# Cross attention and a routed FFN on one core: the query weights are centred before they are folded into the key weights, and the start of the program is put in another order

## The chip, the cores and the metric

The kernel runs on one core of one Trainium2 chip. A core has five engines that run side by side, each through its own queue of instructions in program order: TensorE (PE, matrix products; its weight loads are shown apart as PEld), VectorE (DVE), ScalarE (ACT), GpSimd (POOL) and SyncE (SP, which here only issues DMAs; ACT and POOL issue DMAs too). The metric is the device time of one execution in microseconds (us); smaller is better. All data are float32 unless said otherwise.

## The reference, cut to what matters

```python
def xattn(query, context, w_q, w_kv, w_out, b_out):      # 16 heads of 64
    q = query @ w_q
    k, v = jnp.split(context @ w_kv, 2, axis=-1)
    ...
    attn = jax.nn.softmax(jnp.einsum('bhqd,bhkd->bhqk', q, k) * HEAD_DIM ** -0.5, axis=-1)
    ...
    return out @ w_out + b_out

x = x + xattn(layernorm(x), ctx_768, w_q, w_kv, w_out, b_out)
x = x + moe_ffn(layernorm(x), router_w, w1, w2, w3, sw1, sw2, sw3)
```

`x` is 64 batches of 128 tokens of 128 features, `ctx_768` 64 batches of 77 keys of 96 features, `w_q` 128 x 1024, `w_kv` 96 x 2048. The FFN has eight experts, of which each token takes two, and a shared expert. The layer norm subtracts the mean of a token's 128 features and divides by their deviation.

## The kernel before, in words

**Folded weights.** The kernel never forms q and k. For each head it multiplies the key weights by the query weights once, at the start (`folded`, L231 to L244): `wkq` is 96 x 128 per head, so that keys times `wkq` times the raw tokens gives the scores. The layer norm's mean is taken out of the weights rather than out of the tokens: `fold_keys` (L246 to L259) takes from each row of a folded head its mean over the 128 token features, and scales by 1/8 on the way. The deviation is applied later, as the scale of the exponential (L366). In the same way `fold_values` (L261 to L263) multiplies value weights by output weights. The weights come in two quads `q` of four pairs of heads; a quad is two DMAs (`wk[q]` and `wq[q]`, L104) and 8 products of 64 rows, the even heads into one PSUM bank and the odd heads into another. A float32 product is two PE instructions in the profile. So a quad shows as 16 PE instructions at L237, and on DVE as twice (reduce L250, scale L251, subtract L252), once for each bank; each bank holds 96 x 512.

**Units.** The work on a group of four batches is cut into units of one batch and eight heads. For a unit, `scores` (L343 to L362) multiplies tokens by keys (L351, four PE instructions) into a PSUM tile of two banks that exists once, DVE takes the largest (L360) and subtracts it (L362) and so frees the tile; ACT takes the exponential (L366); DVE sums and inverts (L373, L375) and POOL multiplies (L381 to L385). `keys(k)` makes folded keys for two heads (L334, four PE instructions) and ACT copies them out of PSUM (L341). After that come transposes (L420), products with the values (L403, L430), and the FFN's steps, which are put between the units by a plan written out by hand.

**The start of the program**, which the change touches. SP issues `wk` of both quads, then the first group's keys `cT` (L115), tokens `xg` (L117), transposed tokens `xgT` (L128), and then further inputs and `wo`. ACT issues `wq` of both quads, `wv` of both (L104) and `bo_sb` (L149). POOL makes the identity `ident`, then the constant `mhalf` (L163), then many other constants. The arithmetic then stands in this order for every engine:

```python
    more_constants()
    fold_keys(0)
    fold_keys(1)
    stats(0)
    for k in range(4):
        keys(k)
    start_unit(0, lambda: [keys(k) for k in range(4, 8)])
    start_unit(1, lambda: fold_values(0), lambda: fold_values(1), lambda: residual(0))
```

`stats(0)` is the first group's layer norm statistics on DVE (L277 to L281) and POOL (L283). `start_unit(n, ...)` issues the scores of unit n, then what is handed to it, then the unit's exponential and weights. `keys(0)` to `keys(3)` need the heads 0 to 7, that is both banks of quad 0; `keys(4)` to `keys(7)` need quad 1. ACT loads its function table once ahead of its first arithmetic, a copy at L341.

After the two first units the program goes on unit by unit; further keys, values, FFN and routing work are laid into it, and the last tenth is FFN work on blocks of routed tokens whose inputs and answers go through DRAM.

Of the kernel before, what the change touches and what calls it, by code (L numbers as in the profile page):

```python
# [8 lines left out]
F32 = mybir.dt.float32  # L9
BF16 = mybir.dt.bfloat16  # L10
I32 = mybir.dt.int32
AF = mybir.ActivationFunctionType
ALU = mybir.AluOpType
AX = mybir.AxisListType

B, NQ, D = 64, 128, 128
NKV, DC = 77, 96
# [14 lines left out]
G = 4  # L32
# [30 lines left out]
SCALE = HD ** -0.5  # L63
# [3 lines left out]
def xattn_moe_kernel(  # L67
# [17 lines left out]
    nc = tc.nc  # L85
    PSUM = bass.MemoryType.PSUM

    const = ctx.enter_context(tc.tile_pool(name="const", bufs=1))
    grp = ctx.enter_context(tc.tile_pool(name="grp", bufs=2))
    dram = ctx.enter_context(tc.tile_pool(name="dram", bufs=1, space=bass.MemoryType.DRAM))  # L90
    small = ctx.enter_context(tc.tile_pool(name="small", bufs=3))
# [8 lines left out]
    def weights_of(engine, w, q, n, name):  # L100

        to = ffn.tile([128, WALL], F32, tag="w", name=f"{name}_{q}", bufs=2 * QUAD)
        to = to[:, : 4 * n].rearrange("p (m d) -> p m d", d=n)
        engine.dma_start(out=to, in_=w[:, 4 * q : 4 * (q + 1), :])  # L104
        return to

    wk, wq, wv, wo = {}, {}, {}, {}
    for q in range(2):
        wk[q] = weights_of(nc.sync, wkT, q, DC, "wk")
        wq[q] = weights_of(nc.scalar, wqT, q, D, "wq")  # L110

    def load_inputs(g):
        bs = slice(g * G, (g + 1) * G)
        cT = grp.tile([DC, G, NKV], F32, tag="cT", name=f"cT_{g}", bufs=2)
        nc.sync.dma_start(out=cT, in_=ctxT[:, bs, :])  # L115
        xg = grp.tile([128, G, D], F32, tag="xg", name=f"xg_{g}", bufs=2)
        nc.sync.dma_start(out=xg, in_=x[bs].rearrange("b t d -> t b d"))  # L117
        return xg, cT

    def load_first_keys(g):  # L120

        cM = grp.tile([DC, G // 2, 3 * KM], F32, tag="cM", name=f"cM_{g}", bufs=2)
        nc.sync.dma_start(out=cM, in_=ctxM[:, g * G // 2 : (g + 1) * G // 2, :])
        return cM

    def load_transposed(g):
        xgT = grp.tile([D, T], F32, tag="xgT", name=f"xgT_{g}", bufs=2)
        nc.sync.dma_start(  # L128
            out=xgT.rearrange("d (b t) -> d b t", t=NQ), in_=xT[:, g * G : (g + 1) * G, :]
        )  # L130
        return xgT

    def load_last_keys(g):

        cR = grp.tile([DC, 2 * G * KS], F32, tag="cR", name=f"cR_{g}", bufs=1)
        nc.sync.dma_start(out=cR.rearrange("c (b k) -> c b k", k=KS), in_=ctxR[:, g * G : (g + 2) * G, :])
        return cR

    inputs, transposed = {0: load_inputs(0)}, {0: load_transposed(0)}
    first_keys, last_keys = {0: load_first_keys(0)}, {0: load_last_keys(0)}  # L140
    for q in range(2):
        wv[q] = weights_of(nc.scalar, wvT, q, DC, "wv")
# [13 lines left out]
    def keys_room(name):  # L156

        return grp.tile([D, QUAD * WALL], F32, tag="kx", name=name)

    ident = const.tile([128, 128], F32, name="ident")  # L160
    make_identity(nc, ident)
    mhalf = const.tile([128, G], F32, name="mhalf")
    nc.gpsimd.memset(mhalf, -0.5)  # L163

    ats = []
    for i in range(NAT):
# [24 lines left out]
    def iota(to, pattern, base, step):  # L191
        nc.gpsimd.iota(to, pattern, base=base, channel_multiplier=step, allow_small_or_imprecise_dtypes=True)

    def more_constants():
        for e in range(E):
            nc.gpsimd.memset(rank[:, :, e : e + 1], float(E - e))
        nc.gpsimd.memset(upto, 0.0)
        for e in range(E):
            nc.gpsimd.memset(upto[:, e, : e + 1], 1.0)
            nc.gpsimd.memset(first_row[:, e : e + 1], float(e * rows))  # L200
        iota(block_no, [[1, nb]], 0, 0)
        iota(block_row, [[128, nb]], 0, 1)
        nc.gpsimd.memset(ones, 1.0)
        nc.gpsimd.affine_select(before, ones, [[1, 128]], ALU.is_gt, 0.0, base=0, channel_multiplier=-1)
        iota(dest, [[1, 2 * G]], nb * 128, 2 * G)
        for h in hrs:
            nc.gpsimd.memset(h, 0.0)
        nc.gpsimd.memset(nobody, 0.0)
        nc.gpsimd.memset(nobody[:, D : D + 1], NOWHERE)
        for to in sent:  # L210
            nc.sync.dma_start(out=to[E * rows :, :], in_=nobody)
# [12 lines left out]
    wkq_sb = const.tile([DC, NH, D], F32, name="wkq_sb")  # L224
# [3 lines left out]
    def bank(name, p=128):  # L228
        return ps_g.tile([128, 512], F32, tag="g", name=name)[:p]

    def folded(q, left, right, name):  # L231

        pws = [bank(f"{name}_{q}_{odd}", DC) for odd in range(2)]
        for m in range(4):
            for odd in range(2):
                half = slice(HD * odd, HD * (odd + 1))
                nc.tensor.matmul(  # L237
                    pws[odd][:, m * D : (m + 1) * D],
                    left[q][half, m, :],
                    right[q][half, m, :],  # L240
                    start=True,
                    stop=True,
                )
        return [(slice(8 * q + odd, 8 * (q + 1), 2), pw.rearrange("p (h d) -> p h d", d=D)) for odd, pw in enumerate(pws)]  # L244

    def fold_keys(q):  # L246

        for hs, pw in folded(q, wk, wq, "pwq"):
            mean = small.tile([DC, 4], F32, tag="wmean", name=f"wmean_{hs.start}", bufs=2)
            nc.vector.tensor_reduce(mean, pw, AX.X, ALU.add)  # L250
            nc.vector.tensor_scalar(mean, mean, SCALE / D, None, ALU.mult)  # L251
            nc.vector.scalar_tensor_tensor(  # L252
                wkq_sb[:, hs, :],
                pw,
                SCALE,
                mean.rearrange("p (h o) -> p h o", o=1).broadcast_to([DC, 4, D]),
                ALU.mult,
                ALU.subtract,
            )  # L259

    def fold_values(q):  # L261
        for hs, pw in folded(q, wv, wo, "pwv"):
            nc.scalar.copy(wvo_sb[:, hs, :], pw)  # L263
# [3 lines left out]
    class Norm:  # L267


        def __init__(self, name, src):  # L270
            self.name, self.src = name, src
# [39 lines left out]
    class Attention:  # L311


        def __init__(self, g):
            self.g = g
            self.xg, self.cT = inputs.pop(g)
            self.xgT = transposed.pop(g)
            self.norm = Norm(f"a{g}", self.xg)
            self.kx, self.vo, self.aT, self.sc, self.at = {}, {}, {}, {}, {}

        def residual(self):
            self.x1 = grp.tile([128, G, D], F32, tag="x1", name=f"x1_{self.g}", bufs=NX1)
            nc.gpsimd.tensor_tensor(
                self.x1, self.xg, bo_sb.rearrange("p (o d) -> p o d", o=1).broadcast_to([128, G, D]), ALU.add
            )

        def keys(self, p, i):

            if i == 0:
                self.kx[p] = keys_room(f"kx_{self.g}_{p}")[:, : NH * KP].rearrange("p (h k) -> p h k", k=KP)  # L330
            hs = slice(2 * i, 2 * (i + 1))
            pk = bank(f"pk_{self.g}_{p}_{i}")[:, : 2 * KP].rearrange("p (h k) -> p h k", k=KP)
            for k in range(2):
                nc.tensor.matmul(  # L334
                    pk[:, k].rearrange("p (b k) -> p b k", k=NKV),
                    wkq_sb[:, 2 * i + k, :],
                    self.cT[:, 2 * p : 2 * (p + 1), :],
                    start=True,
                    stop=True,
                )  # L340
            nc.scalar.copy(self.kx[p][:, hs, :], pk)  # L341
# [531 lines left out]
        pairs("values", 4, k)  # L873

    def load_group(g):
        inputs[g] = load_inputs(g)

    def load_first_keys_of(g):
# [8 lines left out]
    for g in range(NG):  # L887
        p = 16 * g
# [24 lines left out]
    g = 0  # L913
# [4 lines left out]
    for g in range(NG - 1):  # L918
        p = 16 * (g + 1)
        routing(g, p, (0, "stats"), (1, "normed"), (3, "transpose"), (4, "logits"), (5, "choose"), (6, "choose_second"))  # L920
    for st in sets:
        for g in range(st.start, min(st.start + st.n, NG - 1)):
            p = 16 * (g + 1)
# [7 lines left out]
    for st in sets[:-1]:  # L931
        p = 16 * (st.start + st.n)
# [6 lines left out]
    for st, after in zip(sets, sets[1:]):  # L939
# [4 lines left out]
        for q, quad in enumerate(quads):  # L944
            p = st.ready + (until - st.ready) * q // (len(quads) - 1)
# [107 lines left out]
    def unit(k):  # L1053
        g, b, t = units[k]
        return attention_of(g), b, t

    def start_unit(k, *between):
        a, b, t = unit(k)
        a.scores(b, t)
        for step in between:  # L1060
            step()
        a.exps(b, t)
        a.weights(b, t)

    more_constants()
    fold_keys(0)
    fold_keys(1)
    stats(0)
    for k in range(4):
        keys(k)  # L1070
    start_unit(0, lambda: [keys(k) for k in range(4, 8)])
    start_unit(1, lambda: fold_values(0), lambda: fold_values(1), lambda: residual(0))
    for k in range(8, 12):
        keys(k)
    load_group(1)
    load_transposed_group(1)
    for i, tag in enumerate(("a", "a", "u", "u")):
# [3 lines left out]
    for k in range(len(units) + 1):  # L1081
# [3 lines left out]
        if k and k % 2 == 0:  # L1085
            a, b, t = unit(k - 1)
# [4 lines left out]
        a, b, t = unit(k)  # L1091
# [87 lines left out]
```

## Time and profile before

| what | value |
|---|---|
| median of 3 runs | 990.72 us (990.32 to 992.84) |
| the profiled execution's own time | 990.29 us |
| its span, first to last instruction | 988.6 us |
| PE / PEld busy | 920.6 us (93%) / 768.4 us (78%) |
| DVE / ACT / POOL busy | 673.3 us (68%) / 651.8 us (66%) / 518.6 us (52%) |
| mean granted TensorE clock | 0.979 of full |
| DMA | 85.76 MB, mean 87 GB/s |

The profiled execution is 1.7 us longer than its span, which is what lies around the first and the last instruction. The page splits the span into 40 slices and gives each engine's busy share of each in tenths. The timeline gives instructions in order of time: start, length in us, engine, line, operation, what it writes and reads, the number of instructions merged into the row, and in brackets how long the engine stood idle before it and what ended that. ACTq and SPq are DMA issues by those engines' queues. The table of groups gives one row for a line and a shape: busy us in all, and mean ns of one instruction, from which an instruction that is new in the program can be priced by its nearest likeness. A mean of one pipelined PE instruction is longer than the step from one to the next; where a step is wanted, it is the length of a merged row divided by its instructions.

### The profile page before, as it was taken

To read this page: it belongs to the slowest core of one execution; us is meant where nothing else is said; L and a number is where in the kernel's file an instruction comes from. 1 tells how busy PE (TensorE), PEld (TensorE's weight loads), DVE (VectorE), ACT (ScalarE), POOL (GpSimd) and SP (SyncE) were. 2 spreads that over 40 slices of the span, in tenths; PEclk is the share of its full clock that TensorE was granted. 3 is DMA by queue.
4 is the path that set the end of the run, shared out by engine and by line. 5 is a ranking of instruction groups with operands and counts; after the bars stand their busy time and mean duration, and the time that the engine had idled before them with its cause. 6 is when DMAs were issued, how large, how long until landed. Compare 5 with 4: busy or idle time off the path is not lost. (4 is left out here: it accounts for less than half of the span.)

```text
span 988.6 us, 18829 instructions
## 1 busy us (share of the span) xinstructions
PE 920.6 (93%) x6103; PEld 768.4 (78%) x6103; DVE 673.3 (68%) x1755; ACT 651.8 (66%) x1417; POOL 518.6 (52%) x688
## 2 busy tenths in 40 slices
PE   7999999999999999999999999999999896689990
PEld 5787877787778878776888888888888775588980
DVE  4566776676767767778686776776676879456552
ACT  4776677676767667675776767666767575456660
POOL 3244563636364544636366375484475556437673
PEclk9999999999999999999999999999999999879995
DMA  5212212212222222122322222123131136623375
GB/s 169 78 59 73 68 41 81 70 54 71 73 70 64 78 70 64 44 88 77 91 76 69 81 84 67 47 84 91 52 95 37 52 111 188 209 61 92 107 221 163
DMA packets 80882, 85.76 MB, mean 87 GB/s; under 512 B 11328, under 2 KB 62912, under 8 KB 80784
## 3 DMA queue, kind: packets, MB, share of 16 engines
q1 hardware_dynamic: 65920, 56.09, 20.7%
q0 software_dynamic: 8864, 18.30, 5.6%
q10 hardware_dynamic: 6000, 10.16, 2.8%
q8 instruction: 49, 0.80, 0.3%
q14 instruction: 49, 0.40, 0.1%
HBM read 48.18 MB, written 36.33 MB: 85 GB/s over the span
## 5 line engine op out<-in xcount | busy, mean ns | idle before, releaser
L334 PEld LDWEIGHTS pk<-cT,wkq_sb 96*128 96x128 f32 x1024 | 157.8, 189 | 70.5 <-issue 42.8
L791 POOL DMA_INDIRECT answers<-y,to x149 | 146.9, 986 | 92.4 <-issue 45.0
L341 ACT COPY kx<-pk 128x308 f32<-128x308 f32 x256 | 104.5, 417 | 129.2 <-PE pk L334 123.9
L334 PE MATMUL pk<-cT,wkq_sb 96*128 96x154 f32 x1024 | 174.9, 294 | 1.4 <-DVE wkq_sb L252 1.0
L351 PE MATMUL ps<-kx,xgT 128*128 128x308 f32 x512 | 156.7, 426 | 11.4 <-DVE sc L362 10.8
L430 PEld LDWEIGHTS py<-vo,aT 128*128 128x128 f32 x1280 | 154.7, 193 | 15.5 <-ACT vo L408 5.3
L430 PE MATMUL py<-vo,aT 128*128 128x128 f32 x1280 | 156.8, 277 | 4.2 <-ACT vo L408 4.0
L629 POOL DMA_INDIRECT sent<-pay,row x128 | 127.2, 994 | 61.7 <-DVE part L619 27.9
L383 POOL TENSOR_TENSOR at<-sc,ri 128x512 f32<-128x512 f32 x64 | 67.3, 1052 | 166.6 <-DVE ri L375 113.0
L408 ACT COPY vo<-pv 64x512 f32<-64x512 f32 x256 | 147.3, 575 | 2.1 <-ACT vn L448 0.4
L403 PE MATMUL pv<-wvo_sb,cM 96*128 96x512 f32 x256 | 131.1, 594 | 1.2 <-DVE hr L507 0.8
L373 DVE TENSOR_REDUCE sm<-sc 128x8 f32<-128x616 f32 x128 | 101.1, 790 | 38.7 <-ACT sc L366 37.8
L366 ACT ACTIVATE sc<-sc,rs_a 128x616 f32<-128x616 f32 x128 | 105.0, 820 | 28.6 <-DVE sc L362 19.6
L351 PEld LDWEIGHTS ps<-kx,xgT 128*128 128x128 f32 x512 | 88.9, 189 | 40.7 <-issue 11.4
L381 POOL TENSOR_TENSOR at<-sc,ri 128x256 f32<-128x256 f32 x128 | 76.8, 623 | 79.3 <-DVE ri L375 31.7
L423 ACT COPY aT<-pa 128x512 f32<-128x512 f32 (+1 forms) x256 | 96.2, 429 | 31.7 <-PE pa L420 27.3
L362 DVE TENSOR_TENSOR sc<-ps,mx 128x616 f32<-128x616 f32 x128 | 102.4, 800 | 12.9 <-DVE mx L360 0.5
L360 DVE TENSOR_REDUCE mx<-ps 128x8 f32<-128x616 f32 x128 | 98.2, 767 | 7.7 <-PE ps L351 6.4
L420 PE MATMUL pa<-ident,at 128*128 128x128 f32 x640 | 92.2, 275 | 0.0
L768 PE MATMUL p<-xT,w 128*128 128x128 f32 x596 | 77.6, 285 | 13.1 <-ACT xT L763 7.2
L768 PEld LDWEIGHTS p<-xT,w 128*128 128x128 f32 x596 | 73.2, 199 | 17.3 <-ACT xT L763 10.1
L420 PEld LDWEIGHTS pa<-ident,at 128*128 128x128 f32 x640 | 75.8, 143 | 11.2 <-issue 10.7
(147 smaller groups left out, 1400.8 us busy)
## 6 DMA issues: line engine op xcount, KB each, us to landing
xb<-sent SPq DMA_DIRECT2D x149, 65.0 KB
last_values<-vn ACTq DMA_DIRECT2D x32, 256.0 KB
vo<-last_values SPq DMA_DIRECT2D x64, 128.0 KB
ya<-answers SPq DMA_DIRECT2D x15, 512.0 KB
xg<-in_x_dram SPq DMA_DIRECT2D x16, 256.0 KB
xgT<-in_xT_dram SPq DMA_DIRECT2D x16, 256.0 KB
parked<-x SPq DMA_DIRECT2D x14, 256.0 KB
yx<-parked SPq DMA_DIRECT2D x14, 256.0 KB
```

What stands on the lines that cost most here:

```text
L334: nc.tensor.matmul(pk[:, k].rearrange("p (b k) -> p b k", k=NKV), wkq_sb[:, 2 * i + k, :], self.cT[:, 2 * p : 2 * (p + 1), :], start=True, ...
L341: nc.scalar.copy(self.kx[p][:, hs, :], pk)
L351: nc.tensor.matmul(ps[:, r, : 4 * NKV].rearrange("p (j k) -> p j k", k=NKV), self.xgT[:, ts], self.kx[p][:, h : h + 4, ks], start=True, st ...
L362: nc.vector.tensor_tensor(at, sc, over_keys(mx), ALU.subtract)
L366: nc.scalar.activation(at, at, AF.Exp, scale=self.norm.rs[:, b : b + 1])
L403: nc.tensor.matmul(pv, self.cM[:, p, KM * r : KM * (r + 2)], wvo_sb[:, h : h + 4, :], start=True, stop=True)
L408: nc.scalar.copy(self.vo[b][rows, 4 * t : 4 * (t + 1), :], pv[rows].rearrange("p (m d) -> p m d", d=D))
L420: nc.tensor.transpose(pa[:, j * NQ : (j + 1) * NQ], keys[:, c : c + 128], ident)
L430: nc.tensor.matmul(py[:, :D], aT[:, m, :], vo[:, m, :], start=(m == 0), stop=(m == NT - 1))
L629: ins = nc.gpsimd.indirect_dma_start(out=sent[st.i], out_offset=bass.IndirectOffsetOnAxis(ap=self.row[:, i : i + 1], axis=0), in_=self.pay ...
L768: nc.tensor.matmul(to[:m, ts], self.w[j][:, c : c + m], self.xT[:, ts], start=True, stop=True)
L791: ins = nc.gpsimd.indirect_dma_start(out=answers[st.i], out_offset=bass.IndirectOffsetOnAxis(ap=self.to[:, j : j + 1], axis=0), in_=self.y ...
```

## The change

1. `wq` is asked for ahead of `wk` in the source (they are on different queues); `mhalf` is made first on POOL, and an exponential of it, whose result nobody reads, is put on ACT's queue between the issues of `wq` and `wv`, so that the table load goes there.
2. On SP's queue the transposed tokens of the first group come ahead of its tokens.
3. A new function `centre(q)` takes the mean out of the query weights before they are folded: reduce, scale and subtract on DVE over 128 x 512 in SBUF, once for each quad. It is the same arithmetic in another place, since the mean of a product's rows is the product with the mean.
4. `fold_keys` then only scales each bank on the way out of PSUM: quad 0 on ACT, quad 1 on DVE.
5. `warm(10)` puts ten products of the identity with itself ahead of the folds on PE; nobody reads them.
6. The fold of quad 1 stands after `keys(0)` to `keys(3)` instead of ahead of them.

```diff
     for q in range(2):
+        wq[q] = weights_of(nc.scalar, wqT, q, D, "wq")
         wk[q] = weights_of(nc.sync, wkT, q, DC, "wk")
-        wq[q] = weights_of(nc.scalar, wqT, q, D, "wq")
+    mhalf = const.tile([128, G], F32, name="mhalf")
+    nc.gpsimd.memset(mhalf, -0.5)
+
+    nc.scalar.activation(small.tile([128, G], F32, tag="shift", name="first_exp"), mhalf, AF.Exp)
...
-    inputs, transposed = {0: load_inputs(0)}, {0: load_transposed(0)}
+    contexts = {0: load_keys(0)}
+    transposed = {0: load_transposed(0)}
+    inputs = {0: load_inputs(0)}
...
+    def centre(q):
+
+        w = wq[q]
+        mean = small.tile([128, 4], F32, tag="wmean", name=f"wmean_{q}", bufs=2)
+        nc.vector.tensor_reduce(mean, w, AX.X, ALU.add)
+        nc.vector.tensor_scalar(mean, mean, 1.0 / D, None, ALU.mult)
+        nc.vector.tensor_tensor(
+            w, w, mean.rearrange("p (m o) -> p m o", o=1).broadcast_to([128, 4, D]), ALU.subtract
+        )
+
     def fold_keys(q):
-
         for hs, pw in folded(q, wk, wq, "pwq"):
-            mean = small.tile([DC, 4], F32, tag="wmean", name=f"wmean_{hs.start}", bufs=2)
-            nc.vector.tensor_reduce(mean, pw, AX.X, ALU.add)
-            nc.vector.tensor_scalar(mean, mean, SCALE / D, None, ALU.mult)
-            nc.vector.scalar_tensor_tensor(
-                wkq_sb[:, hs, :],
-                pw,
-                SCALE,
-                mean.rearrange("p (h o) -> p h o", o=1).broadcast_to([DC, 4, D]),
-                ALU.mult,
-                ALU.subtract,
-            )
+            if q == 0:
+                nc.scalar.mul(wkq_sb[:, hs, :], pw, SCALE)
+            else:
+                nc.vector.tensor_scalar(wkq_sb[:, hs, :], pw, SCALE, None, ALU.mult)
+
+    def warm(n):
+
+        pi = bank("pi")
+        for _ in range(n):
+            nc.tensor.matmul(pi[:, :128], ident, ident, start=True, stop=True)
...
     more_constants()
+    warm(10)
+    for q in range(2):
+        centre(q)
     fold_keys(0)
-    fold_keys(1)
     stats(0)
     for k in range(4):
         keys(k)
+    fold_keys(1)
     start_unit(0, lambda: [keys(k) for k in range(4, 8)])
```

The rest of the diff splits `load_inputs` into a load of keys and a load of tokens; the later groups call the two one after the other, in the order they had.

## Prediction, made before the changed kernel was run

> **What bounds the kernel now.** I read the page's busy shares and 40 slices first, then PE's waits, then the timeline of the first 20 us, because all edits lie there.
>
> ```profile
> PE 920.6 (93%) x6103; PEld 768.4 (78%) x6103; DVE 673.3 (68%) x1755; ACT 651.8 (66%) x1417; POOL 518.6 (52%) x688
> PE   7999999999999999999999999999999896689990
> ```
>
> PE is nine tenths busy or more from the second slice to the 31st. In the waits of PE between 16 and 400 us there is one row:
>
> ```profile
> PE ps L351 <- DVE sc L362: 0.4, 1, 0.4
> ```
>
> This is the wait that ends at 16.02 us. From there PE never waits for another engine before 400 us, so the start counts by the moment at which PE gets there, unit 1's scores, and the work of PE behind that moment is unchanged. What the start gains is carried to the end, unless a later wait is fixed by something else. Later waits exist (PE waits 13 us in 400 to 800 us, 23 us in 800 to 990), but most of them are for engines that PE's own products feed, so I let them move along. The timeline of the start (start, length, engine, line, in brackets the idle time before):
>
> ```profile
> 4.85 3.63 PE L237 MATMUL pwq<-wq,wk 64*96 64x128 f32 x32 [4.85 <-DMA wk<-in_wkT_dram]
> 6.90 0.69 DVE L250 TENSOR_REDUCE wmean<-pwq 96x4 f32<-96x512 f32 x1 [6.90 <-PE pwq L237]
> 7.23 0.33 ACTq L149 DMA_DIRECT2D bo_sb<-in_b_out_dram  x1
> 7.60 1.28 ACT L341 ACT_TABLE_LOAD   x1 [7.60 <-DMA cT<-in_ctxT_dram]
> ...
> 10.09 2.10 PE L334 MATMUL pk<-cT,wkq_sb 96*128 96x154 f32 x14 [0.99 <-DVE wkq_sb L252]
> 10.65 1.99 ACT L341 COPY kx<-pk 128x308 f32<-128x308 f32 x4 [1.77 <-PE pk L334]
> ...
> 14.24 0.79 DVE L360 TENSOR_REDUCE mx<-ps 128x8 f32<-128x616 f32 x1
> 15.07 0.80 DVE L362 TENSOR_TENSOR sc<-ps,mx 128x616 f32<-128x616 f32 x1
> 16.02 1.28 PE L351 MATMUL ps<-kx,xgT 128*128 128x308 f32 x4 [0.44 <-DVE sc L362]
> 17.23 1.99 PE L237 MATMUL pwv<-wo,wv 64*96 64x128 f32 x32
> ```
>
> The reader is to see a chain: weights at 4.85, fold of quad 0 (2.05 to DVE's first reduce), two banks on DVE to 10.03 (3.13), keys from 10.09, their copies, scores to 13.48, then DVE. DVE has quad 1 and the statistics in hand until 14.33, so the maximum starts at 14.24 and the PSUM tile is free at 15.87.
>
> **Part by part, with the new chain.**
>
> Centring adds, for each quad, a reduce, a small scale and a subtract on DVE. The 96x512 reduce took 0.68 (L250), the scale 0.17 (L251), an SBUF 128x512 add 0.70 (L833); from start to start the old trio took 0.73 + 0.20, so 0.73 + 0.20 + 0.70 = 1.62. From 4.85 that ends at 6.47. The trace shows only that both first weight DMAs had landed at 4.85; if `wq` alone landed earlier the start is earlier. Quad 1 is centred to 8.0, beside PE and off the path.
>
> Fold 0 starts at 6.53 (DVE's end to PE's start took 0.06 at 10.03). Its price is the question of `warm`. The same 32 instructions took 3.63 us at 4.85 and 1.99 us at 17.23:
>
> ```profile
> L237 PE MATMUL pwq<-wq,wk 64*96 64x128 f32 x32 | 3.6, 418 | 4.8 <-DMA wk<-in_wkT_dram 4.8
> L237 PE MATMUL pwv<-wo,wv 64*96 64x128 f32 x32 | 2.0, 274 | 0.0
> ```
>
> That is a step of 0.107 against 0.056. The view by stretches gives a granted clock of 1.00 in both, so the slowness of the first instructions is seen in their durations alone. The shortest of the early ones, 317 ns, comes only at 8.2; PE runs slowly for some 3.4 us after its first product. Ten identity products are 20 instructions. The nearest warm row is L430 (128 columns, 20 in 2.39 us, a step of 0.11); times 0.107/0.056 that is 0.21, so 20 take 4.3 us. `ident` is ready at 1.36, so they run from about 1.45 to 5.75 and cost nothing: DVE's centring to 6.47 covers them. I take it that fold 0 is then fast: 16 instructions, 15 x 0.056 + 0.27 = 1.1, to 7.64 (the even bank 7.53). Bounds: slow, 1.9, to 8.4.
>
> The Trainium skill ("TensorE: Matmul & The Clock Gate", Part 1) says that PE runs at half clock until an activity window of about 3.4 us was busy, and that the windows run free of the kernel's start. The trace agrees in size. But by that rule the identity products may straddle two windows and then pause for 0.8 us, and the rule speaks against this change; that is the second rival.
>
> Scaling quad 0 moves to ACT: a 96x512 copy out of PSUM took 0.59, four in 2.04 (L263), a step of 0.48. Moving the table load ahead (1.28 us) hides it in ACT's idle start; before it hid behind the wait to 10.65, so by itself it gives nothing, but in the new order ACT is wanted at 7.55, and without the move it would end at 8.88. Between stand ACT's issues of `wv` and `bo_sb`, the last of which ended at 7.56. These are slow because ACT's queue waits to issue (the first `wv` at 1.70, the second only at 5.76, `bo_sb` at 7.23); `wv` now goes behind table and exponential, at about 3.3, while `wq` is still moving, so I leave 7.56. So the scales run 7.60 to 8.68. Keys of head 1 then start at 8.73 against 10.09: 1.36 gained. Copies end at 12.64 - 1.36 = 11.28.
>
> On PE the keys last to 10.83; fold 1, new in this place, takes its 1.1 us now on the path (10.67 to 11.78; before it lay beside DVE's work). So scores of unit 0 run 11.57 to 12.78 (1.21 without the old ACT stall, as at 26.50), against 13.48. Of the 1.36 only 0.70 is left.
>
> DVE then scales quad 1: two 96x512 from PSUM; bounds 0.42 (a 128x624 copy in SBUF, 0.51) and 0.69 (L252), I take 0.65 because reads of PSUM all took about that. They run 11.77 to 13.0; the statistics are done by then, at 9.3 if `xg` has landed. `xg` now follows `xgT`. All that is ahead of it or beside it is 1.95 MB, and the DMAs moved 0.88 MB by 5 us and 323 GB/s after, which makes about 8.3 us, an estimate; DVE is there at 7.95, and the slack to 11.77 covers it. The maximum starts at 13.0, the subtraction ends 1.63 later, at 14.63. Keys 4 to 7 start at 13.0 and take 2.1 on PE, so its instructions are out at about 14.95, and unit 1's scores start there against 16.02. The stall of 0.44 is gone; PE's own key products come in its place. Their copies and the exponential of unit 0 end only 0.4 sooner, but ACT then idles 1.6 before L263, which covers that.
>
> The sum: 16.02 - 14.95 = 1.07, say **1.05 us** for what is off the end. Against the profiled execution, 990.29 (988.6 of span and 1.7 around it), that is 989.24; the median of the runs is 0.43 higher. I take the middle of the two for the base, 990.5, and predict **989.5**. About 0.3%, 3 us, is what a measurement of this kernel can tell from no change.
>
> **Rivals.**
>
> *No gain from the start beyond a little.* If fold 0 stays slow, it ends 0.75 later; keys then follow with it, and 0.3 is left: 990.2. For it speaks the pause, against it the 4.3 us of product before it. If `wq` lands sooner, ACT's 7.56 still binds, and at most 1.9 is gained: 988.6.
>
> *ACT is held by its DMA issues.* If `wv`, now issued later, pushes `bo_sb` behind by the 1.5 us that table and exponential take, the scales run to 10.2, keys start 0.1 late, and fold 1 adds its place on PE: 0.4 slower, 990.9. For: ACT's issues waited 3.6 and 1.1 us in this very place. Against: `wv` queues behind `wq` either way.
>
> *Slower: the identity products in series.* If each of the 20 waits for the one ahead of it (same bank, same weights), the step isn't 0.21 but a load and a product whole, 0.28 + 0.42 = 0.70 by the slow rows. Then PE is free at 15.4, not 5.75, fold 0 starts 8.9 late, and the time is 989.5 + 8.9 = 998.4. It begins to cost at a step of 0.25 and outweighs the gain at 0.31. Against it: products into one bank follow each other at 0.11 at L430.
>
> *A late wait falls in another way.* PE's waits behind 400 us are few and single (longest 5.9, 4.0, 3.6, 2.2). If the shift frees one, 2 to 6 more are gained, 983.5 to 987.5; it could also add one.
>
> **How the numbers follow.** Forecast 0.48, slow fold or earlier `wq` 0.19, ACT held 0.08, series 0.08, a late wait freed 0.13, a late wait added 0.04. Faster by over 0.3% is the freed wait: 0.13. Slower by over 0.3% is series and the added wait: 0.12. The rest, 0.75, is within. The range goes from the greatest start gain with a little of the freed waits, 987.6, to ACT held plus the runs' own scatter (medians of a few runs between 990.3 and 990.9), 991.6.
>
> **What would show it.** Right: 20 identity instructions done before 6.5; L237 of fold 0 at about 274 ns; ACT's first scale at 7.6; keys from 8.7; unit 1's scores at about 15.0 and no PE wait from there to 400 us; the same distance from there to the end. Wrong: identity products beyond 6.5, ACT issuing DMAs beyond 7.6, DVE waiting for `xg` beyond 11, or a wait on PE behind 400 us that differs by 2 us or more.

## The result, and the profile after

| | before | after |
|---|---|---|
| median of 15 runs each | 990.77 us (987.59 to 995.24) | 988.01 us (985.15 to 990.04) |
| ratio, 95% interval | | 0.9966 [0.9952, 0.9981] |
| profiled execution / its span | 990.29 / 988.6 us | 985.48 / 983.8 us |

The kernel became 3.4 us faster by the ratio (1.9 to 4.7), 2.8 by the medians. 1.05 had been predicted: the direction is as forecast, the gain about three times as large. The page of the changed kernel, its busy shares and PE's 40 slices:

```profile
PE 924.1 (94%) x6123; PEld 771.5 (78%) x6123; DVE 671.4 (68%) x1751; ACT 652.8 (66%) x1420; POOL 517.4 (53%) x688
PE   8999999999999999999999999999999987779990
```

PE has 20 instructions more (the identity products), DVE four fewer, ACT three more. The slices differ at the first, where the identity products are, and at 32 to 36, some 770 to 890 us. The start of the changed kernel from its timeline, PE, PEld, ACT and DVE (start, length, engine, line, idle time before):

```profile
1.45 4.19 PE L273 MATMUL pi<-ident 128*128 128x128 f32 x20 [1.45 <-POOL ident masks.py:199]
...
6.32 1.12 PE L243 MATMUL pwq<-wq,wk 64*96 64x128 f32 x16 [0.67 <-DVE wq L258]
...
7.46 1.08 ACT L265 ACTIVATE wkq_sb<-pwq 96x512 f32<-96x512 f32 x2 [4.26 <-PE pwq L243]
8.11 2.58 PE L348 MATMUL pk<-cT,wkq_sb 96*128 96x154 f32 x16 [0.68 <-ACT wkq_sb L265]
8.59 1.87 PEld L348 LDWEIGHTS pk<-cT,wkq_sb 96*128 96x128 f32 x14 [0.19 <-ACT wkq_sb L265]
...
8.77 0.87 DVE L291 BATCH_NORM_STATS2 st_a<-xg 128x6 f32<-128x128 f32 x4 [0.99 <-DMA xg<-in_x_dram]
...
10.62 1.12 PE L243 MATMUL pwq<-wq,wk 64*96 64x128 f32 x16
...
11.77 1.28 DVE L267 TENSOR_SCALAR wkq_sb<-pwq 96x512 f32<-96x512 f32 x2 [1.64 <-PE pwq L243]
...
13.02 0.80 DVE L374 TENSOR_REDUCE mx<-ps 128x8 f32<-128x616 f32 x1
13.86 0.80 DVE L376 TENSOR_TENSOR sc<-ps,mx 128x616 f32<-128x616 f32 x1
15.04 1.46 PE L365 MATMUL ps<-kx,xgT 128*128 128x308 f32 x4
...
15.71 0.30 PEld L365 LDWEIGHTS ps<-kx,xgT 128*128 128x128 f32 x2 [0.47 <-ACT kx L355]
```

The reader is to see the predicted chain link by link: fold 0 fast (1.12), the scales at 7.46, the keys of head 0 at 8.11 and those of head 1 at 8.59 (the weights' row of PEld; 8.73 was predicted), fold 1 on the path from 10.62, the maximum at 13.02, unit 1's scores at 15.04 (predicted 14.95) against 16.02. From there to 400 us PE's products wait for no other engine; only two of its weight loads still wait, at 15.71.

So the start is as predicted. The rest of the gain is behind it. I took the moment at which PE comes to the same instruction in both traces: the changed kernel is ahead by 0.80 us at 20 us, 0.78 at 400, 1.05 at 800, 0.6 at 870, 2.2 at 876 and 3.3 at 890; its span ends 4.8 sooner. Below, "shift" is this lead or lag at 100 us (minus is sooner), against the trace of before shown above.

### The profile page after: what moved, and what is told of

It reads as the page before. It is cut to its first block, busy times and chain, and to the rows that moved or that the text cites. A ratio compares the mean times of both kernels' runs of the same rounds, so it can differ in the third digit from the quotient of the medians.

```text
span 983.8 us, 18867 instructions
## 1 busy us (share of the span) xinstructions
PE 924.1 (94%) x6123; PEld 771.5 (78%) x6123; DVE 671.4 (68%) x1751; ACT 652.8 (66%) x1420; POOL 517.4 (53%) x688
## 4 chain that ended last, share of the span: by engine, by line
PE 69%; DVE 10%; ACT 9%; DMA 5%; issue 4%; SPq 2%; POOL 1%; ACTq 0%; DVEq 0%; POOLq 0%
PE py L444 13%; PE ps L365 11%; PE pk L348 11%; PE pv L417 8%; PE pa L434 5%; PE p L782 4%; PE p_s L654 3%; PE pn L454 2%; PE ph L782 2%; PE pq L794 2%; PE pq L795 2%; DMA answers<-y,to 2%; PE pf L667 1%; PE pf L666 1%; DMA out_dram<-yx 1%
```

## The experiments

**Is the rest bound to a place in time, or to the program?** Theory T: what comes late depends on when the start releases it, so the kernel before, delayed or not, shows the same. Theory M: the changed program has a gain of its own. Theory S: nothing but the start, and the rest is scatter. Both kernels ran again, and the changed one with idle identity products that delay everything behind the start.

```diff
+    warm(4)        # d_after_p4; warm(12) in d_after_p12
     for k in range(8, 12):
         keys(k)
```

> The kernel before, unchanged, timed against itself: it gives the measurement's own scatter and a second profile of the same program. Every theory expects 0 us within about 1.5 us of the median. Theory S (only the start has changed, and its gain is carried to the end one for one) expects the second profile to have the same stretch from 17 us to the end within 1 us. Theory T (the last 160 us lose more or less time by where PE's slow stretches fall) expects that stretch to differ by 2 us or more between two profiles of one program.

> The changed kernel again. Theory S expects 0.8 us less than before in the median, and a profile whose shift is -0.8 us both at 17 us and at the end. Theory M (something that the change leaves behind shortens the end) and theory T expect 2.5 to 4 us less, of which 0.8 at 17 us and the rest behind 800 us.

> The changed kernel with 4 more products of the identity (8 PE instructions of about 0.11 us, 0.9 us) where PE is never idle, at about 18 us, ahead of keys 8 to 11: the start's gain is given back and nothing else is changed. Theory S: 0.1 us more than the kernel before. Theory M: 0.9 us more than the changed kernel, so still some 2 us less than the kernel before. Theory T: what is gained behind 800 us is drawn anew; between 2 us less and 2 us more than before, and not the changed kernel's time plus 0.9.

> The same with 12 products more (24 PE instructions, 2.7 us). Theory S: 1.9 us more than the kernel before. Theory M: 2.7 us more than the changed kernel, which is about the time of the kernel before. Theory T: not on the straight line through the changed kernel and the one with 4 products, by 1.5 us or more.

Then the kernel before was delayed too, by repeating the last values' first product two or three times more, and the changed one in the same way; one more changed kernel has no identity products at all. Repeated products write the same values again.

```diff
-            nc.tensor.matmul(...)
+            for _ in range(3 if (g, i) == (0, 0) else 1):   # 4 in b_d3
+                nc.tensor.matmul(...)
```

```diff
-    warm(10)       # p_no_warm
```

> The kernel before with one product at 22 us (values_of_last, L440, 128x512, two PE instructions of 0.43 us) made three times instead of once, into the same bank: PE, which is never idle there, comes 1.7 us later to everything behind it, and nothing else is changed. If only the moment counts one for one (theory S) or the changed program carries a fixed gain of its own that this one lacks (theory M): 1.7 us more than the kernel before, a median near 992.6. Theory T (the slow stretches of PE begin and end on a grid of 3.41 us that lies much the same in every run, between 0.8 and 1.7 us after the first instruction in six profiles, so that the end loses more or less by where it falls on that grid): the part behind 800 us is about 1.5 us shorter, so 0 to 0.6 us more than the kernel before.

> The same with that product made four times: 2.6 us later. S and M: 2.6 us more than the kernel before, near 993.5. Theory T: 2.6 us later is the changed kernel's place on the grid of 3.41 us (it is 0.8 to 1.0 us early, and 3.41 - 0.9 = 2.5), so the part behind 800 us is about 2 us shorter and the time 0.3 to 1.1 us more than before, near 991.5. A difference of 2 us between the theories, with 0.5 us of uncertainty.

> The changed kernel with the same product made three times: 1.7 us later, so 0.8 us behind the kernel before at 25 us. M: the changed kernel's time plus 1.7, near 989.5. Theory T: a place on the grid between those of the kernels with 4 and 12 products, where the fixed gain need not hold: 990 to 991.5. S: 991.7.

> The changed kernel without the ten products of the identity. All theories on the start: fold 0 starts as in the changed kernel or up to 0.1 us sooner, but is slow, 16 instructions in 1.9 us instead of 1.1, so keys and unit 1's scores come about 0.7 us later than in the changed kernel, and 0.1 us ahead of the kernel before. By S 0.1 us less than before; by T a place on the grid like that of the kernel with 4 products, 1 to 1.5 us less than before; by M, if what it leaves behind is the PSUM bank that these products take, the kernel before's time, and else some 2 us less.

All times against the kernel before on the same chip; the difference in us is the ratio less one, times 990; the rest is difference less shift.

| kernel | ratio [95%] | difference | shift | rest |
|---|---|---|---|---|
| `c_before` | 0.9991 [0.9978, 1.0005] | -0.9 | -0.2 | -0.7 |
| `b_d2` | 1.0012 [0.9997, 1.0027] | +1.2 | +1.8 | -0.6 |
| `b_d3` | 1.0026 [1.0009, 1.0042] | +2.6 | +2.4 | +0.2 |
| changed, first run | 0.9966 [0.9952, 0.9981] | -3.4 | -0.8 | -2.6 |
| `c_after` | 0.9973 [0.9958, 0.9988] | -2.7 | -1.0 | -1.7 |
| `d_after_p4` | 0.9984 [0.9969, 0.9999] | -1.6 | -0.1 | -1.5 |
| `a_d2` | 0.9985 [0.9967, 1.0003] | -1.5 | +0.9 | -2.4 |
| `p_no_warm` | 1.0002 [0.9986, 1.0019] | +0.2 | +2.2 | -2.0 |
| `d_after_p12` | 0.9998 [0.9985, 1.0011] | -0.2 | +2.4 | -2.6 |

The three runs of the program before have a rest of -0.4 in the mean, the six of the changed program -2.1. Each is uncertain by about 1.4, the difference of the means by about 1, and the shift is that of one execution. At the same shift of 2.4 `b_d3` is 2.6 slower and `d_after_p12` is level with before. T put `b_d3` at about 991.5 and it came to 993.6; S asked for no gain beyond the shift. Both fall; M stands in these runs: some 1.7 us go with the program, wherever in time it is put.

`p_no_warm` also settles what the identity products are for. PE's timeline of it:

```profile
5.97 2.03 PE L243 MATMUL pwq<-wq,wk 64*96 64x128 f32 x16 [5.97 <-DVE wq L258]
8.67 4.47 PE L348 MATMUL pk<-cT,wkq_sb 96*128 96x154 f32 x16 [0.68 <-ACT wkq_sb L265]
13.08 1.69 PE L243 MATMUL pwq<-wq,wk 64*96 64x128 f32 x16
...
18.08 1.46 PE L365 MATMUL ps<-kx,xgT 128*128 128x308 f32 x4
```

Without them fold 0, all 16 key products and most of fold 1 are slow (4.47 against 2.58 us for the keys), and unit 1's scores come at 18.08 instead of 15.04. They are worth 3.0 us at unit 1's scores, not the 0.75 at which I priced a slow fold; the expectation ahead of this run had 0.7.

**Is the rest the halving of PE's clock in late waits?** The trace's clock records show why a wait can cost more than itself. The granted clock is 1.00 or 0.50 and changes only on a grid of 3.41 us, whose place differs from run to run. Stretches of `b_d3` and, after it, of the kernel before (stretch, its length, busy time and instructions of PE, PEld, DVE, ACT and POOL, then PEclk, DMA share and GB/s):

```profile
460.00:465.00 5.00, 4.61 (x27) 3.15 (x25) 4.72 (x11) 1.63 (x4) 3.20 (x4) 1.00 0.52 102
465.00:470.00 5.00, 3.35 (x10) 2.60 (x10) 4.73 (x9) 2.27 (x4) 4.23 (x6) 0.61 0.29 96
470.00:475.00 5.00, 5.00 (x28) 4.52 (x28) 2.28 (x5) 1.65 (x4) 0.90 (x2) 0.71 0.32 76
```

```profile
460.00:465.00 5.00, 2.95 (x15) 1.84 (x14) 4.69 (x11) 1.84 (x4) 2.79 (x6) 1.00 0.55 136
465.00:470.00 5.00, 5.00 (x35) 4.30 (x34) 4.76 (x9) 3.53 (x9) 3.33 (x4) 1.00 0.06 16
```

PE has the same two waits in both, 0.40 and 1.65 us, near 461 and 463 before and near 463 and 466 in `b_d3`, but in `b_d3` the clock is halved from 466.1 to 472.9, and it loses 2.9 us between 400 and 600 us. So identity products were put into that wait, and then into two waits of the tail as well, in both kernels.

```diff
+        if k == 79:
+            warm(6)                 # "fill462" and "fill"
...
-        2: [last("transpose"), last("logits")],
+        2: [last("transpose"), lambda: warm(8), last("logits")],    # "fill" only
...
+            if k == 0:
+                warm(8)             # "fill" only
```

> The kernel before with six products of the identity in the 1.65 us for which PE waits at 462 us (12 PE instructions of 0.11 us, 1.3 us, so they end ahead of what it waits for). Theory C (the changed kernel's fixed gain is that PE's clock is halved less often at this wait: PE's busy share of a clock window there is 0.48 to 0.59, at the edge, and two of four profiles of this program and its delayed forms lost 1.5 and 2.9 us to it, none of six of the changed one): 0.8 to 1.5 us less than the kernel before. Theory M elsewhere (the gain lies in the last 160 us): no change, within 0.5 us.

> The changed kernel with the same six products at the same place. Theory C: the changed kernel's time, within 0.5 us, and so a difference of 1.0 to 1.8 us to the kernel before with them. Theory M: a difference of 2.5 to 3 us between the two as without them.

> The kernel before with those six products and eight each in two waits of the last part: ahead of the first product of the first block of the end (PE waits 1.5 and 5 us there for transposed tokens and copied weights) and ahead of the router's product of the last group (PE waits 3.6 us for ACT's copy). PE keeps its full clock there, or gets it back sooner. Theory T (the last 160 us lose by the halved clock behind such waits): 1.5 to 3.5 us less than with the first six alone. If the clock there costs nothing because DMAs set the end: no change.

> The changed kernel with all 22 products. Theory T: 1 to 3 us less than the changed kernel, and 0.8 to 1.3 us less than the kernel before with the 22, which is the start's gain and little else, since the clock's part is now the same in both. Theory M in the last part by something else than the clock: still 2.5 to 3 us less than the kernel before with the 22.

These four ran on a chip on which every kernel took 5% longer (before: 1039.3), so only their ratios are given: 0.9999 [0.9974, 1.0024], 0.9975 [0.9956, 0.9995], 0.9969 [0.9946, 0.9992] and 0.9982 [0.9966, 0.9999]. The clock was halved at other places as well (near 587 us in all four). Theory M does not show there: with six products the changed program is 2.5 us ahead, but its start is 2.5 ahead too (shifts of -1.0 and +1.5), and with all 22 it is 1.3 us behind though its start is 1.9 ahead (-0.5 and +1.4). With an uncertainty of some 3 us for each pair, and so many more halvings, this does not refute M, but it limits it to the other chips. Three of the four ran again on another chip.

> The kernel before with six products of the identity in PE's wait at 462 us, on another chip than the first time (there every kernel took 5% longer, with waits of its own kind). Theory C (the kernel before loses time in some of its runs because its wait at 462 us halves PE's clock): 0.8 to 1.5 us less than the kernel before. If the changed kernel's fixed gain lies elsewhere: within 0.5 us.

> The kernel before with the 22 products in three waits (462 us and two in the last part). Theory T with C (all of the gain behind the start is PE's clock): 2 to 3.5 us less than the kernel before. No effect of the clock: within 0.5 us.

> The changed kernel with the same 22 products. T with C: 0.5 to 1.3 us less than the kernel before with the 22, the start's gain alone, because the clock no longer differs; 3 to 4.5 us less than the kernel before. If the changed program has a gain of another kind: 2.5 to 3 us less than the kernel before with the 22.

| kernel | ratio [95%] | difference | shift | rest |
|---|---|---|---|---|
| `n_b462` | 0.9997 [0.9984, 1.0010] | -0.3 | -0.2 | -0.1 |
| `n_b_fill` | 0.9982 [0.9968, 0.9997] | -1.8 | -0.3 | -1.5 |
| `n_a_fill` | 0.9964 [0.9952, 0.9976] | -3.6 | -0.3 | -3.3 |

Filling the wait at 462 us alone does nothing that can be told, against 0.8 to 1.5 us expected. Against the mean rests above, filling all three waits is worth about 1.1 us to either program, and between the two 1.8 us are left, uncertain by 1.9. So the halvings that these products take away are not shown to be the difference; the runs speak rather against it. In the two profiled executions of this pair the lead behind the start is nearly the same at 900 us (1.93 before, 2.05 changed); at the end the changed program is 1.0 ahead.

**Which edit carries it?** One kernel leaves the early exponential out, so that ACT's table load is late again; one folds quad 1 directly behind quad 0; the last has the early fold and all three fills.

```diff
-    nc.scalar.activation(small.tile(..., name="first_exp"), mhalf, AF.Exp)     # p_no_table
```

```diff
     fold_keys(0)
+    fold_keys(1)      # p_fold_early, q_best
     stats(0)
     for k in range(4):
         keys(k)
-    fold_keys(1)
```

> The changed kernel without the early exponential, so that ACT's table load stands again ahead of its first arithmetic, the scale at L264 of this file. Leaves out an exponential that nobody reads; the computation is whole. Start: the load begins behind the last DMA issue at about 7.5 and ends at about 8.8, so the two scales run 8.8 to 9.9 instead of 7.46 to 8.54; keys, fold 1 and unit 1's scores come about 1.3 later, at 16.3 against 15.04; unless ACT's issues, no longer behind the load, end sooner. Theory 'the start alone, one for one': about +0.3 to +0.5 against the kernel before, as the start gain of 0.8 to 1.0 is gone. Theory 'the changed program has about 1.8 us of its own, at any shift': -1.3 to -1.8 against the kernel before, about 989. Theory 'the part moved on ACT is what gives the 1.8': about 0 to +0.5 as with the first.

> The changed kernel with the fold of quad 1 back ahead of the keys, as it was. On the start: fold 1 runs beside ACT's scales of quad 0, DVE's scales of quad 1 end near 9.5 us, and the scores of unit 0 come about 1 us sooner than in the changed kernel, since 16 PE instructions leave the path; but DVE's scales stand ahead of the statistics no longer. Unit 1's scores, which wait for the subtraction: 0.5 to 1.2 us sooner than in the changed kernel, so 1.5 to 2 us ahead of the kernel before. The whole: 0.5 to 1.2 us less than the changed kernel.

> The changed kernel with both later edits together: fold 1 directly behind fold 0, and identity products in the three PE waits that stood at the edge of the halved clock (6 instructions' worth ahead of one unit near 462 us, 8 in each of two waits of the tail). The reference's computation is whole. Each by itself came to about 3.6 and 3.8 us below the kernel before. If they add (fold 0.3 to 0.5 sooner, fills about 1): -4.0 to -5.0 us, about 986; if the fills only took what the grid of the clock would have given anyway: -3.6 to -3.8, as each alone. If products in the waits are in PE's way: above -3.

| kernel | ratio [95%] | difference | shift | rest |
|---|---|---|---|---|
| `p_no_table` | 0.9995 [0.9978, 1.0013] | -0.5 | +1.7 | -2.2 |
| `p_fold_early` | 0.9967 [0.9955, 0.9979] | -3.3 | -1.3 | -2.0 |
| `q_best` | 0.9946 [0.9927, 0.9966] | -5.3 | -1.8 | -3.5 |

The time of `p_no_table`, uncertain by 1.75, can't tell its three expectations apart. Its start is not 1.3 later than the changed kernel's but 2.5, which is 1.7 behind the kernel before. Its fold 1, from PE's timeline, and the clock around it, from the stretches:

```profile
12.31 1.95 PE L242 MATMUL pwq<-wq,wk 64*96 64x128 f32 x16
```

```profile
12.00:14.30 2.30, 2.30 (x19) 1.79 (x18) 0.01 (x1) 0.42 (x1) 0.00 (x0) 0.55 0.66 127
```

PE stood still from 7.7 to 9.0 us for the late scale, the clock was halved, and fold 1 took 1.95 instead of 1.12. The rest of the gain stayed, so nothing points to the early table load as what carries it. `p_fold_early` brings unit 1's scores to 14.52, 0.52 sooner. That is half of the 1.05 that fold 1 had cost on the path, because the keys now stand behind it and start at 8.93 instead of 8.11. In its time (0.9967 against 0.9966 and 0.9973) nothing of this shows, where 0.5 to 1.2 us were expected; its profile has a halved clock at 462.9. `q_best` is the fastest: 985.29 us median against 989.68, 4.4 us by the medians and 5.3 by the ratio. The centring of the query weights, the scaling on ACT and the order of the DMAs were not taken back one by one.

**Where the two programs differ behind the start.** I compared every engine's step from one instruction to the next in all these traces. Up to 835 us a few steps differ by 0.2 to 1.0 us, and nearly always between programs, not between runs. ACT, kernel before, changed kernel, and `p_no_table`, at the copy behind a DMA issue:

```profile
448.71 0.33 ACTq L449 DMA_DIRECT2D last_values<-vn  x1
449.07 0.75 ACT L423 COPY aT<-pa 128x512 f32<-128x512 f32 x2 [0.40 <-PE pa L420]
```

```profile
447.94 0.33 ACTq L463 DMA_DIRECT2D last_values<-vn  x1
448.59 0.75 ACT L437 COPY aT<-pa 128x512 f32<-128x512 f32 x2 [0.68 <-PE pa L434]
```

```profile
450.47 0.33 ACTq L462 DMA_DIRECT2D last_values<-vn  x1
450.83 0.75 ACT L436 COPY aT<-pa 128x512 f32<-128x512 f32 x2 [0.40 <-PE pa L433]
```

ACT stands 0.28 longer here (0.32 from the issue's end to the copy against 0.04) in all eleven profiles of programs with the early exponential, and neither in the eight of the program before and its variants nor in `p_no_table`. The copy waits for the same things in all. What follows is on DVE, POOL and PE, before and then changed:

```profile
455.07 0.83 DVE L705 TENSOR_TENSOR c<-block_no,last 128x640 f32<-128x640 f32 x1
456.79 1.85 DVE L708 TENSOR_TENSOR c<-c,blocks 128x640 f32<-128x640 f32 x1
...
455.17 1.55 POOL L629 DMA_INDIRECT sent<-pay,row  x1 [0.30 <-issue]
456.74 1.21 POOL L381 TENSOR_TENSOR at<-sc,ri 128x256 f32<-128x256 f32 x2
...
461.04 1.12 PE L403 MATMUL pv<-wvo_sb,cM 96*128 96x512 f32 x2 [0.40 <-DVE u_s L488]
```

```profile
454.59 1.31 DVE L719 TENSOR_TENSOR c<-block_no,last 128x640 f32<-128x640 f32 x1
456.78 0.84 DVE L722 TENSOR_TENSOR c<-c,blocks 128x640 f32<-128x640 f32 x1
...
455.23 1.71 POOL L395 TENSOR_TENSOR at<-sc,ri 128x256 f32<-128x256 f32 x2
...
460.02 1.13 PE L417 MATMUL pv<-wvo_sb,cM 96*128 96x512 f32 x2
```

Before, both of POOL's products of 128 x 256 lie beside the second of these DVE operations; in the changed kernel one of them lies beside the first. The first is then 0.48 longer and the second 1.01 shorter. PE's wait at 461.04 for `u_s` (0.40) is gone, and PE gains 0.25 us, in these programs alone; `p_no_table` has 0.82 and 1.85 and no such gain. That ACT's 0.28 sets this off is read from its coming and going together in all profiles; no run moved it alone. DVE has places of the same kind. In the tail, before and changed:

```profile
865.79 0.68 DVE L488 SCALAR_TENSOR_TENSOR u<-a,p 128x512 f32<-128x512 f32 x1
866.95 0.69 DVE L489 TENSOR_TENSOR h<-u,p 128x512 f32<-128x512 f32 x1 [0.47 <-DVE u L488]
```

```profile
864.46 0.68 DVE L502 SCALAR_TENSOR_TENSOR u<-a,p 128x512 f32<-128x512 f32 x1
865.24 0.69 DVE L503 TENSOR_TENSOR h<-u,p 128x512 f32<-128x512 f32 x1
```

Before the change DVE stands 0.47 ahead of `h`, for nothing but its own last result; after it, 0.10. It is 0.47 in all eight profiles of the program before and its variants, and 0.10 in all twelve of the changed program and its variants, `p_no_table` among them, however they are shifted. In the changed kernel the chain of work that ended last runs through this very stretch:

```profile
865.24 0.69 DVE h L503
...
867.60 0.49 ACT pay L305
...
872.93 0.48 ACT x2T_f L318
873.45 1.06 PE pl L553 x8
```

So 0.37 us of the lead arise on the way to PE's products at 873. The changed program has such a pause of 0.46 elsewhere instead, at 651 us, where PE does not feel it.

**Where the pauses stand.** Number everything that the trace has for an engine in order of time, with DMA issues, register operations and recorded waits. DVE's pause ahead of `h` then stands at record 1984 before, its pause at 651 us in the changed kernel at record 1472, and ACT's pauses at 172 and 448 us in the changed kernel at records 320 and 832. Each number is 64 more than a multiple of 128, in every profile that has the pause. With four DVE records fewer, or with ACT's three more, another instruction comes to such a place; with ACT's exponential taken away again (`p_no_table`) both ACT pauses go and DVE's stay as in the changed kernel. At many such places no pause is seen.

## Why the prediction was wrong

*What bounds the start, and its price: right.* Identity products: done at 5.64 (5.75 predicted), step 0.21 as estimated. Fold 0: 1.12 (1.1). ACT's scales: from 7.46 (7.60), released by fold 0 and not by ACT's last DMA issue, which had ended at 7.40. Fold 1 on the path: 1.12. DVE's scales of quad 1: 1.28 for two, as I took. Unit 1's scores: 15.04 (14.95), behind PE's own key products as forecast, 0.98 sooner than before. Their second half then waited for ACT's copies of the keys (PE's weights stood idle for 0.47 ahead of 15.71), so the lead at 20 us is 0.80 and not 1.05. The weights also landed at 4.64 us in this execution (DVE's first reduce) and at 4.85 in the one of before, so 0.2 of the lead, and part of the match with 14.95, is luck. Carried to 400 us the lead is 0.78, so "from there to 400 us" held.

*Slow fold: the chance was real and the price too low.* It is the first of the rivals, though the prediction refers to it as the second. With this same start, unit 1's scores came at 15.04, 14.84, 14.86, 15.07, but at 15.59 and 15.58 in two profiles, where the identity products met the clock's grid badly and fold 0 took 1.82 and 1.58. The mean gain of these six profiles against six of before is 0.72 at the scores, and 0.54 at PE's next products, behind ACT's copies: about half of the 1.05. The Trainium skill ("TensorE: Matmul & The Clock Gate", Part 1) says that the clock is set by windows of 3413 ns that run free of the kernel's start; the traces agree: edges 3.41 us apart, and the first full clock between 4.3 and 7.6 us with the identity products. What I missed is that a slow fold is not the end of it: `p_no_warm` stayed at half clock until 14.3.

*The wrong rivals.* ACT was not held: `bo_sb` was issued by 7.40. The products did not run in series. `xg` landed at 8.77 (8.3 estimated), and DVE then still waited 1.64 for fold 1.

*The step that failed* is "the work of PE behind that moment is unchanged. What the start gains is carried to the end ... so I let them move along". The work is the same, but its steps are not. 1.7 to 1.8 us of the gain, uncertain by about 1, are not the start moving through; on every chip but the slow one they go with the changed program at any shift from -1.8 to +2.4 us. Of these the traces show 0.25 at 461 us (it comes and goes with ACT's 0.28, by way of DVE and POOL) and 0.37 at 867 us (DVE's pause ahead of `h`, on the chain). About 1.1 stay open. Over the six profiles of before and its variants and the ten of the changed one, the slow chip left out, the mean lead behind the start differs by 0.0 at 450 us, 0.8 at 470 (0.5 of it from halvings near 466 us in three profiles), 1.3 at 890 and 1.9 at the end. Single profiles scatter by 1 to 2 us, but about 0.6 of the open part arise behind 900 us, and what sets them has not been followed. In the two traces compared the lead grows by 1.2 between 876 and 890 us, where the halved clock lasts to 882.1 before and to 878.9 after:

```profile
870.00:880.00 10.00, 6.45 (x38) 6.21 (x37) 4.48 (x11) 7.49 (x18) 2.84 (x3) 0.76 0.16 40
```

```profile
870.00:880.00 10.00, 7.57 (x54) 7.33 (x53) 5.05 (x11) 8.22 (x17) 4.17 (x4) 0.83 0.17 46
```

In both, PE is busy throughout the first slow window (from 875.2 and from 875.4), yet before the change a second slow one follows. The window ahead of it had PE busy for 3% before and for 58% after. An earlier 0.37 may decide such things, which would turn it into more, but the fills removed this halving from both programs and 1.8 between them stayed; it is not shown. That the pauses hang on an instruction's place in its engine's queue is shown by their places above; what the engine does there is not. The rival "a late wait falls in another way" came nearest, with the wrong reason: no wait was freed by the shift. The direction was forecast for the start alone; that the rest added to it rather than took from it was luck. The predicted time also leaned on medians of few runs: before itself ran from 987.6 to 995.2.

## What to carry to other kernels

Price the start of a program in PE's slow time, and keep PE busy without a gap from its first product until the clock is full; here ten products that nobody reads were worth 3.0 us. Check what must follow the moment that you price: here ACT's copies took back 0.2 of the 0.98. A change of a few instructions at the start can shift fixed pauses on the engines that execute them, hundreds of us later: a saving of less than some 2 us can't be forecast by moving the rest along, and both ends of the range should allow for it. To tell such an effect from the start's own gain, delay both kernels by idle work and compare them at the same shift.

## What the runs showed of the hardware

- The granted clock is 1.00 or 0.50, and every change in these traces lies on a grid of 3.41 us whose place against the first instruction differs from profile to profile. With the slow chip left out, slow windows that were followed by a full one had PE busy for 84% and more; 81% and 80% were not enough (`d_after_p12` from 0.8 us, `p_no_warm` from 7.5). It does not always suffice: in six profiles, the one of before among them, a slow window that began between 875 and 879 us, with PE busy for 98% and more, was followed by another slow one. A full clock was mostly halved behind a window in which PE was busy for 51% or less, with exceptions on both sides (67% in `b_d3` at 879.1, halved; 48% in `n_b_fill` at 871.7, not halved).
- PEclk says 1.00 for the first microseconds, though the instructions there take about twice as long (a step of 0.107 against 0.056 in the kernel before); the first record of a clock comes only with the first full window, there at 8.26 us.
- A table load of 1.28 at 1.71 us was followed by its exponential at 3.00, 0.01 behind its end.
- DVE and ACT pause by 0.28 to 0.41 us ahead of certain instructions. The pause is tied to the program and not to the time: the same in every profile of one program, at another instruction when a few instructions had been taken out or added far ahead of it. The four followed here stand at an engine's records 320, 832, 1472 and 1984, all 64 more than a multiple of 128.
- A DVE operation of 128 x 640 took 0.83 us with an indirect DMA of POOL beside it and 0.84 with POOL's product of 128 x 104 (456.91 in the changed kernel); it took 1.31 with one POOL product of 128 x 256 beside it and 1.85 with two.
